# A diagonal LSTM and a small quantum-circuit layer: chunks that come back as one buffer per image, and one store cut into nine

## The chip, the cores and the metric

The kernel runs on one core of one Trainium2 chip. The metric is the device time in microseconds (us) of one execution, the median of three runs. A core has five engines that run their own instruction streams: PE (TensorE, matmuls), DVE (VectorE), ACT (ScalarE), POOL (GpSimd) and SP (SyncE, which here only issues transfers). Transfers between DRAM and the on-chip memory are carried out by 16 DMA engines that serve all issuing queues; here SP's queue (hardware descriptors) and POOL's queue (software descriptors) are used.

## The reference, cut to what matters

The input is x of shape 16 images, 128 channels, 64 by 64, in float32. Layer 0 is a diagonal LSTM over a skewed image, layer 1 a per-pixel map with four angles and a fixed 16-state circuit; both have a group norm ahead of them and a residual around them.

```python
# layer 0: rows are shifted against each other, then scanned column by column
x = x + _L0_conv_ref(_gn(x), w_is, b_is, w_ss, b_ss)
# layer 1, for each pixel of _gn(x):
def _L1_conv_ref(x, pre_w, pre_b, q_weights, post_w, post_b):
    N, C, H, W = x.shape
    xf = x.transpose(0, 2, 3, 1).reshape(-1, C)
    xq = xf @ pre_w.T + pre_b              # 128 channels -> 4 angles
    z = _simulate(xq, q_weights)           # 4 numbers per pixel
    out = z @ post_w.T + post_b            # 4 -> 128 channels
    return out.reshape(N, H, W, -1).transpose(0, 3, 1, 2)
x = x + _L1_conv_ref(_gn(x), pre_w, pre_b, q_weights, post_w, post_b)
```

## The kernel before

**Layout.** The 128 channels lie on the 128 partitions. An image is cut into eight chunks of 512 columns (8 rows of 64, 2 KB per partition, 256 KB per chunk), numbered k = 0 to 7. Layer 0 keeps the state of all 16 images in `ring`, which has room for only 40 of the 64 rows of each image. While the scan runs, the finished rows 0 to 23 of every image (chunks k = 0, 1, 2, "low" chunks) are therefore written to a DRAM buffer `low` and their place in `ring` is filled with later rows of x. Chunks k = 3 to 7 are still in `ring` when layer 1 starts; the 48 low chunks (three for each of 16 images) have to come back.

**Layer 1.** `finish` (L1158) ends every chunk: DVE adds the output of the last matmul, a bias and the chunk itself (L1167, in place), and SP stores the result to `out` (L1173). The main loop goes over images b = 1 to 15 (image 0 is done in halves ahead of it). In an iteration PE makes the outputs of the lower half (k = 0 to 3), DVE finishes them, ACT and DVE turn the angles of image b + 2 into sines (`sines`, L1115 to L1120), PE makes `squares` of image b + 1 and the outputs of the upper half (k = 4 to 7), DVE finishes these, and PE makes the angles of image b + 3 (`angles`, L1099), which read all eight chunks of that image in the order k = 4, 6, 2, 0, 5, 7, 3, 1. So the low chunks of image 15 are needed at the end of iteration 12. PE's outputs go through five PSUM banks.

**Loads.** `places` is a list of free chunk buffers. At first it has eight scratch buffers of the scan (`spare`, the first three of them one tile `trio`) and seven new ones (`low0` to `low6`): 15 chunks, images 0 to 4. Eight of them are loaded by SP in the last scan steps (`low_rows`, L983), seven by POOL. After that every chunk that `finish` is through with gives its buffer to the list, chunks of `ring` too; `load(3)` is called after each half image, takes up to three buffers and issues a load of one chunk each on POOL's queue. With two calls per image, 48 chunks have been asked for by the end of image 5. A load may only start when the store that empties its buffer has landed.

**Stores.** `together` (L1176) says how many chunks go out in one store: low chunks singly, k = 3 singly, and the upper chunks two at a time for images 1 to 3, four at a time (1 MB, 8 KB per partition) after that; image 15 goes out in single chunks. All stores stand in SP's queue in program order. Each also waits for the semaphore of the transfer eight before it, so that at most eight of SP's transfers are under way.

Of the kernel before, what the change touches and what calls it, by code (L numbers as in the profile page):

```python
# [11 lines left out]
F32 = mybir.dt.float32  # L12
# [4 lines left out]
P = 128  # L17
NB = 16
# [6 lines left out]
ROWS = 4  # L25
BLOCK = ROWS * NW
CHUNK = 2 * BLOCK
# [4 lines left out]
FEW = 96  # L32
TWICE = 128
LEAST = 128
AHEAD = RING - SLOTS
BAND = NW + 1
NSTEP = BAND + NW + SLOTS - 1
# [45 lines left out]
def kernel(  # L83
# [16 lines left out]
    nc = tc.nc  # L100
    xv = x.rearrange("b c h w -> b c (h w)")
    ov = out.rearrange("b c h w -> b c (h w)")

    const = ctx.enter_context(tc.tile_pool(name="const", bufs=1))
# [6 lines left out]
    ring = const.tile([P, NB, RING * NW], F32, name="ring")  # L111
    NLOW = NH - RING
    NT = NLOW * NW // CHUNK
    low = dram.tile([NB, P, NLOW * NW], F32, name="low")
# [11 lines left out]


    trio = const.tile([P, 3, CHUNK], F32, name="trio")
    spare = [trio[:, i] for i in range(3)]
    spare += [const.tile([P, CHUNK], F32, name=f"spare{i}") for i in range(3, 8)]  # L130
    w_theta = const.tile([P, 128], F32, name="w_theta")
    w_image = const.tile([P, NB, 48], F32, name="w_image")
    b_image = const.tile([P, NB], F32, name="b_image")
# [5 lines left out]
    def place(r):  # L139

        return (r + AHEAD if r < SLOTS else r - SLOTS) * NW

    def block(r):

        return ring[:, :, place(r) : place(r) + BLOCK]
# [18 lines left out]
    with ExitStack() as scan:  # L164
# [55 lines left out]
        def above(v, a, b):  # L220

            v = v[:, 1, 0:1]
            dims = [list(v.ap[0]), [NB - NC, 2], [1, b - a]]
            return bass.AP(v.tensor, v.offset + a - NB, dims)
# [8 lines left out]
        with ExitStack() as prep:  # L233
# [25 lines left out]
            def rows(b):  # L259
                half = SLOTS // 2  # L260
                first = 0 if b else AHEAD
                early = ((first, half - first), (half, half))
                for r, n in (*(early if b < 3 else ((0, SLOTS),)), (SLOTS, AHEAD)):
                    nc.sync.dma_start(
# [6 lines left out]
            def behind(b):  # L271
# [10 lines left out]
                out=qw, in_=q_weights.rearrange("l w a -> (l w a)").partition_broadcast(P)  # L282
            )
            nc.sync.dma_start(out=ring[:, 0, place(0) : place(AHEAD)], in_=xv[0, :, 0 : AHEAD * NW])
            for i in range(2):
# [146 lines left out]
            def cleared():  # L432
                for v in (*hst, *xns, none, cst[:, :, 0:LEAST]):
                    nc.gpsimd.memset(v, 0.0)
                    yield
                nc.gpsimd.memset(eps, EPS)
                nc.gpsimd.tensor_sub(apart_of, ident, group)
                yield
                nc.gpsimd.memset(w_image, 0.0)
                yield  # L440
# [60 lines left out]
            for g in ORDER:  # L501
                first[g] = ps_gate.tile([P, 2, NC], F32, name=f"ps0_{g}", tag="gate")
                for w, rhs in ((w1T, hst[0][:, :, 0 : LEAST // 2]), (w0T, above(hst[0], 0, LEAST // 2))):
                    nc.tensor.matmul(
                        first[g][:, :, 0 : LEAST // 2],
                        lhsT=w[:, g * 128 : (g + 1) * 128],
# [106 lines left out]
        def reach(t):  # L613

            b = columns(t)[1]
            return b + 4 if b < NC else b

        def plain(t):
            a, b = columns(t)
            return b - a <= FEW  # L620
# [5 lines left out]

        def wide(t, least=LEAST):

            a, b = columns(t)[0], reach(t)
            return max(0, min(a, b - least)), max(b, min(NC, a + least))  # L630

        def diagonal(t, band, q, j0, j1):


            r = 2 * j0 + q + AHEAD * (1 - band)
            at = r * NW + t - BAND * band - 2 * j0 - q
# [15 lines left out]
        def apart(op, *groups):  # L652

            for key in groups:
                tc.declare_no_dep(op.ins, group=key, reason="other rows of the ring")
            return op

        def ahead_of(op, band, j1):

            apart(op, "stores", *(f"reload{g}" for g in reloads if band == 0 or 2 * j1 <= AHEAD + 4 * g))  # L660

# [24 lines left out]
        def gate_ps(t):  # L686

            a, b = wide(t, LEAST // 2)
            ps = {} if t else first
# [172 lines left out]
        def step(t, ps):  # L862

            a, b = columns(t)
            few = plain(t)
            a0, b0 = wide(t, LEAST // 2 if few else LEAST)
            w = reach(t)
# [112 lines left out]
        def low_rows(queue, n, v):  # L980
            b, k = n // NT, n % NT
            of = low[b, :, k * CHUNK : (k + 1) * CHUNK]
            queue.dma_start(out=v, in_=of)  # L983

        waiting = []
        with tc.manual_schedule():
# [26 lines left out]
            v = block(NH - ROWS).rearrange("p i (r w) -> p i r w", w=NW)[:, :, :, NW - STRIP :]  # L1013
# [4 lines left out]
            for i, u in enumerate((d, sq)):  # L1018
                u = u.rearrange("p i r w -> p i (r w)")
# [33 lines left out]
    lowp = ctx.enter_context(tc.tile_pool(name="lowp", bufs=1))  # L1053
# [8 lines left out]

    places = list(spare) + [lowp.tile([P, CHUNK], F32, name=f"low{i}") for i in range(7)]
    lows = []

    def load(n):

        while n and places and len(lows) < NT * NB:  # L1070
            v = places.pop(0)
            lows.append(v)
            if len(lows) > 8:
                low_rows(nc.gpsimd, len(lows) - 1, v)
            n -= 1

    def rows_of(b, k):
        if k < NT:
            return lows[NT * b + k]
        at = place(2 * ROWS * k)  # L1080
        return ring[:, b, at : at + CHUNK]

    def half(v, c):

        if c is None:
            return v
        return v[:, c * BLOCK : (c + 1) * BLOCK]
# [71 lines left out]
    def finish(b, h, po, c=None):  # L1159
        for j in range(4):  # L1160
            k = 4 * h + j
            v = rows_of(b, k)
            x1, y, o = half(v, c), po[j], ov[b, :, k * CHUNK : (k + 1) * CHUNK]
            to = v
            if c is not None:
                o, to = o[:, c * BLOCK : (c + 1) * BLOCK], x1
            nc.vector.scalar_tensor_tensor(to, y, b_out, x1, ALU.add, ALU.add)  # L1167
            n = together(b, k) if c is None else 1
            if (k + 1) % n == 0:
                if n > 1:  # L1170
                    at = place(2 * ROWS * (k + 1 - n))
                    o, to = (u[:, at0 : at0 + n * CHUNK] for u, at0 in ((ov[b], (k + 1 - n) * CHUNK), (ring[:, b], at)))
                nc.sync.dma_start(out=o, in_=to)  # L1173
            if c is None or c == 1 and k < NT:
                places.append(v)

    def together(b, k):

        if k < 4 or b == NB - 1:
            return 1  # L1180
        return 2 if b < 4 else 4

    def idle():
# [4 lines left out]
            nc.tensor.matmul(ps, lhsT=w_out, rhs=v, start=True, stop=True)  # L1188

    with tc.manual_schedule():  # L1190
        load(len(places))

        angles(0, 0)
        angles(0, 1, bank(ps_o, "theta0"))
        first = [sines(0, c) for c in range(2)]
        for later in first:
            next(later)

        th = bank(ps_t, "theta1")
        angles(1, 0, th)  # L1200
        for later in first:
            next(later, None)
        squares(0, 0)
        angles(1, 1, th, (0,))
        po = outputs(0, 0, 0)
        angles(1, 1, th, (1,))
        ths[1, None] = th
        finish(0, 0, po, 0)
        squares(0, 1)
        po = outputs(0, 1, 0)  # L1210
        finish(0, 1, po, 0)
        later = sines(1)
        next(later)
        po = outputs(0, 0, 1, (0, 1))
        th = angles(2, parts=(0,))
        po += outputs(0, 0, 1, (2, 3))
        finish(0, 0, po, 1)
        next(later, None)
        po = outputs(0, 1, 1, (0,))
        angles(2, None, th, (1,))  # L1220
        later = sines(2, by=nc.gpsimd)
        next(later)
        load(3)
        po += outputs(0, 1, 1, (1,))
        squares(1)
        po += outputs(0, 1, 1, (2, 3))
        finish(0, 1, po, 1)
        next(later, None)
        for b in range(1, NB):
            po = outputs(b, 0)  # L1230
            if b == 1:
                angles(3)
            later = sines(b + 2, by=nc.gpsimd if b == 1 else nc.vector) if b + 2 < NB else iter(())
            if b == 1:
                next(later)
            finish(b, 0, po)
            load(3)
            if b == 1:
                po = outputs(b, 1)
                finish(b, 1, po)  # L1240
                load(3)
                squares(2)
                next(later, None)
                angles(4)
                continue
            next(later, None)
            if b + 1 < NB:
                squares(b + 1)
            next(later, None)
            po = outputs(b, 1)  # L1250
            finish(b, 1, po)
            load(3)
            if b + 3 < NB:
                angles(b + 3)
            elif b < NB - 1:
                idle()
# [37 lines left out]
```

## Time and profile before

| | us |
|---|---|
| median of 3 runs (lowest, highest) | 1400.34 (1399.78, 1400.67) |
| the profiled execution, its own time | 1399.66 |
| its span, first to last instruction | 1397.8 |
| layer 1, from the first angles matmul to the end of the span | 1277.0 to 1397.8 |
| images 5 to 14, one iteration | 6.33 |
| last DVE instruction ends | 1386.7 |

Over the span PE is busy for 97%, DVE for 70%, ACT for 56%, POOL for 64%. These are averages over two layers with different limits; the change lies in the last 9% of the span. Times inside the kernel are counted from the start of the span, so the run's own time lies about 1.9 us above them. "DMA share" is the mean busy share of the 16 DMA engines; it can stand a little over 1, since a packet's record overlaps the next one's by a few ns. "To landing" is the time from the start of a transfer's issue to the last of its semaphore writes.

### The profile page before, as it was taken

How to read it: one execution, taken by the hardware profiler on the slowest of the kernel's cores; microseconds unless marked ns; L12 is line 12 of the kernel's file. 1: busy time of each engine (PE TensorE's matmuls, PEld its weight loads, DVE VectorE, ACT ScalarE, POOL GpSimd, SP SyncE). 2: the span in 40 equal slices, each digit the busy share in tenths (PEclk: the TensorE clock that was granted, in tenths of full speed). 3: DMA queues.
4: the chain of work that ended last, by engine and by line, in shares of the span. 5: the costliest groups of instructions: out<-in, count | busy, mean ns of one | idle time of the engine just before them, and what ended most of it. 6: DMA issues, size and time to landing. Idle time of an engine off the chain costs nothing. (4 is left out here: it accounts for less than half of the span.)

```text
span 1397.8 us, 19939 instructions
## 1 busy us (share of the span) xinstructions
PE 1351.0 (97%) x6058; PEld 966.6 (69%) x6058; DVE 973.6 (70%) x2520; ACT 786.3 (56%) x1881; POOL 892.6 (64%) x1584
## 2 busy tenths in 40 slices
PE   7789999999999999999999999999999999989996
PEld 6668887777777777767777767777777778886332
DVE  6973565577767775677777776666665566876996
ACT  6765666555555555555555555555555566644331
POOL 3236777766677777777777766777777667764400
PEclk9999999999999999999999999999999999999998
DMA  9940000000000000133333100000000000014998
GB/s 373 417 199 1 2 1 1 1 1 1 1 1 1 1 1 1 60 121 121 121 121 120 61 1 1 1 1 0 1 1 1 1 0 1 1 31 144 382 415 354
DMA packets 52746, 107.02 MB, mean 77 GB/s; under 512 B 3824, under 2 KB 31504, under 8 KB 49568
## 3 DMA queue, kind: packets, MB, share of 16 engines
q1 hardware_dynamic: 49024, 95.17, 18.3%
q0 software_dynamic: 3472, 10.58, 2.0%
q8 instruction: 48, 0.79, 0.2%
q14 instruction: 58, 0.48, 0.1%
q10 hardware_dynamic: 144, 0.01, 0.0%
HBM read 59.61 MB, written 46.14 MB: 76 GB/s over the span
## 5 line engine op out<-in xcount | busy, mean ns | idle before, releaser
L693 PE MATMUL ps<-spare,wxT 128*128 128x512 f32 (+18 forms) x1280 | 479.6, 518 | 0.6 <-POOL spare L684 0.6
L887 DVE TENSOR_TENSOR ps<-ps,both 128x256 f32<-128x256 f32 (+9 forms) x536 | 219.8, 410 | 295.5 <-PE ps L872 291.1
L891 ACT ACTIVATE ps<-ps,bias 128x512 f32<-128x512 f32 (+23 forms) x480 | 279.2, 583 | 219.5 <-DVE ps L887 183.1
L693 PEld LDWEIGHTS ps<-spare,wxT 128*128 128x128 f32 x1280 | 230.9, 190 | 173.2 <-issue 155.5
L872 PE MATMUL ps<-trio,w1T 128*128 128x256 f32 (+14 forms) x1088 | 306.3, 363 | 0.0
L872 PE MATMUL ps<-trio,w0T 128*128 128x256 f32 (+14 forms) x1088 | 305.5, 362 | 0.0
L922 ACT COPY both<-ps 128x256 f32<-128x256 f32 (+9 forms) x536 | 189.6, 356 | 181.0 <-PE ps L872 161.5
L872 PEld LDWEIGHTS ps<-spare,wsT 128*128 128x128 f32 x1088 | 196.0, 190 | 78.8 <-DVE spare L957 30.4
L872 PE MATMUL ps<-spare,wsT 128*128 128x256 f32 (+14 forms) x1088 | 243.6, 365 | 1.6 <-DVE spare L957 1.3
L730 POOL TENSOR_TENSOR ring<-ring,spare 128x256 f32<-128x256 f32 (+15 forms) x375 | 231.4, 643 | 18.3 <-DVE spare L957 18.0
L872 PEld LDWEIGHTS ps<-trio,w1T 128*128 128x128 f32 x1088 | 201.6, 190 | 22.3
L872 PEld LDWEIGHTS ps<-trio,w0T 128*128 128x128 f32 x1088 | 201.1, 190 | 21.2
L684 POOL TENSOR_TENSOR spare<-spare,rstd 128x512 f32<-128x512 f32 (+10 forms) x160 | 170.9, 1068 | 14.2 <-DVE rstd L528 1.7
L678 POOL TENSOR_TENSOR spare<-ring 128x256 f32<-128x256 f32 (+13 forms) x165 | 139.4, 845 | 0.0
L951 ACT ACTIVATE g<-cst 128x256 f32<-128x256 f32 (+20 forms) x320 | 103.0, 368 | 64.2 <-DVE cst L950 63.6
L957 DVE TENSOR_TENSOR spare<-g,ps 128x256 f32<-128x256 f32 (+17 forms) x319 | 105.3, 367 | 44.3 <-ACT g L951 39.4
L720 POOL TENSOR_TENSOR trio<-spare 128x240 f32<-128x240 f32 (+9 forms) x136 | 102.5, 754 | 36.7 <-DVE spare L957 33.1
L672 POOL TENSOR_TENSOR spare<-ring,mean 128x256 f32<-128x256 f32 (+15 forms) x191 | 122.5, 641 | 2.5 <-DVE mean L517 2.0
L891 ACT ACTIVATE g<-ps,bias 128x512 f32<-128x512 f32 (+20 forms) x160 | 97.3, 608 | 27.6 <-DVE ps L887 21.3
L950 DVE TENSOR_TENSOR cst<-cst,ps 128x256 f32<-128x256 f32 (+20 forms) x320 | 104.5, 368 | 5.5
L947 DVE TENSOR_TENSOR ps<-ps,g 128x512 f32<-128x512 f32 (+20 forms) x160 | 95.1, 594 | 18.7 <-ACT g L891 18.5
L939 DVE TENSOR_TENSOR cst<-cst,ps 128x512 f32<-128x512 f32 (+20 forms) x160 | 92.7, 579 | 16.5 <-POOL spare L231 10.9
(385 smaller groups left out, 1172.3 us busy)
## 6 DMA issues: line engine op xcount, KB each, us to landing
ring<-in_x_dram SPq DMA_DIRECT2D x13, 1024.0 KB, 9.8
low<-ring SPq DMA_DIRECT2D x6, 2048.0 KB, 7.6
ring<-in_x_dram SPq DMA_DIRECT2D x6, 2048.0 KB, 8.2
out_dram<-ring SPq DMA_DIRECT2D x11, 1024.0 KB, 9.1
out_dram<-ring SPq DMA_DIRECT2D x37, 256.0 KB, 7.2
trio<-in_x_dram SPq DMA_DIRECT2D x7, 768.0 KB, 7.6
rest<-in_x_dram SPq DMA_DIRECT2D x7, 768.0 KB, 7.8
ring<-in_x_dram SPq DMA_DIRECT2D x18, 256.0 KB, 9.9
```

Source lines behind the costliest of these rows:

```text
L672: op = nc.gpsimd.tensor_sub(by_pairs(xn, 0, j0, j1), x0, over(mean1, j1 - j0))
L678: op = nc.gpsimd.tensor_sub(by_pairs(xn, 1, j0, j1), lower, of)
L684: nc.gpsimd.tensor_mul(v, v, r)
L693: nc.tensor.matmul(ps[g][:, :, a:b], lhsT=wxT[:, g * 128 : (g + 1) * 128], rhs=xns[t % 2][:, :, a:b], start=t > 0, stop=True, skip_group_c ...
L730: op = engine.tensor_add(x1, x1, by_pairs(new, q, j0, j1))
L872: nc.tensor.matmul(out, lhsT=w[:, g * 128 : (g + 1) * 128], rhs=rhs, start=False, stop=True, skip_group_check=True,)
L887: nc.vector.tensor_add(v, v, both[g][:, a:b])
L891: nc.scalar.activation(to[:, :, a:w], ps[g][:, :, a:w], FUNC[g], bias=bias[:, g : g + 1])
L922: nc.scalar.copy(both[g][:, a:b], ps[g][:, 0, a:b])
L950: nc.vector.tensor_add(c[:, q], c[:, q], ig[:, q])
L951: nc.scalar.activation(th[:, q, a:w], c[:, q], AF.Tanh)
L957: nc.vector.tensor_mul(new[:, q, a:v], th[:, q, a:v], act[GO][:, q, a:v])
```

## The change

The scratch buffers are regrouped: five buffers for three chunks each (`trio`, a second `trio1`, `pair` and `last`, and two new tiles `low0` and `low1`), each holding the low chunks of one image. The place of a buffer is handed on as a whole, image b's to image b + 5, when `finish` is through with k = 2 of image b; `ring` chunks are no longer given away. A load brings three chunks at once (6 KB per partition), or two and one for `pair` and `last`; the calls of `load()` after each half image remain, but find at most one free group per image. Low chunks of images 2 to 14 are stored with their buffer, three at once (or two and one). The upper store of image 11 (`EASED`), 1 MB, isn't issued when its chunks are ready: it is cut into nine accesses, the p-th of partitions p, p + 9, p + 18, ... (two of 15 partitions, seven of 14), and one of them is issued behind each of the next nine stores, those of images 12 to 14.

```diff
+EASED = NB - 5
+APART = 9
-    spare = [trio[:, i] for i in range(3)]
-    spare += [const.tile([P, CHUNK], F32, name=f"spare{i}") for i in range(3, 8)]
+    trio1 = const.tile([P, 3, CHUNK], F32, name="trio1")
+    pair = const.tile([P, 2, CHUNK], F32, name="pair")
+    spare = [v[:, i] for v, n in ((trio, 3), (trio1, 3), (pair, 2)) for i in range(n)]
...
-    places = list(spare) + [lowp.tile([P, CHUNK], F32, name=f"low{i}") for i in range(7)]
-    lows = []
-    def load(n):
-        while n and places and len(lows) < NT * NB:
-            v = places.pop(0)
-            lows.append(v)
-            if len(lows) > 8:
-                low_rows(nc.gpsimd, len(lows) - 1, v)
-            n -= 1
+    later = [lowp.tile([P, NT, CHUNK], F32, name=f"low{i}") for i in range(2)]
+    last = lowp.tile([P, CHUNK], F32, name="last")
+    first_lows = spare + [last] + [v[:, i] for v in later for i in range(NT)]
+    groups = {i: [(v, NT)] for i, v in ((0, trio), (1, trio1), (3, later[0]), (4, later[1]))}
+    groups[2] = [(pair, 2), (last.unsqueeze(1), 1)]
+    freed, loaded, parted = [], [len(groups)], []
+    def load():
+        while freed and loaded[0] < NB:
+            b = loaded[0]
+            groups[b] = freed.pop(0)
+            k = 0
+            for v, n in groups[b]:
+                of = low[b, :, k * CHUNK : (k + n) * CHUNK]
+                nc.gpsimd.dma_start(out=v, in_=of.rearrange("p (k n) -> p k n", n=CHUNK))
+                k += n
+            loaded[0] += 1
+    def low_group(b, k):
+        for v, n in groups[b]:
+            if k < n:
+                return v, n, k
+            k -= n
...
             n = together(b, k) if c is None else 1
-            if (k + 1) % n == 0:
+            if (k + 1) % n == 0 if k >= NT else n == 1 or n == low_group(b, k)[2] + 1:
                 if n > 1:
-                    at = place(2 * ROWS * (k + 1 - n))
-                    o, to = (u[:, at0 : at0 + n * CHUNK] for u, at0 in ((ov[b], (k + 1 - n) * CHUNK), (ring[:, b], at)))
-                nc.sync.dma_start(out=o, in_=to)
-            if c is None or c == 1 and k < NT:
-                places.append(v)
+                    o = ov[b, :, (k + 1 - n) * CHUNK : (k + 1) * CHUNK]
+                    if k < NT:
+                        o, to = o.rearrange("p (k n) -> p k n", n=CHUNK), low_group(b, k)[0]
+                    else:
+                        at = place(2 * ROWS * (k + 1 - n))
+                        to = ring[:, b, at : at + n * CHUNK]
+                if n > 1 and k >= NT and b == EASED:
+                    pieces = [(o[p::APART], to[p::APART]) for p in range(APART)]
+                    parted.extend(pieces)
+                else:
+                    nc.sync.dma_start(out=o, in_=to)
+                    if parted:
+                        o, to = parted.pop(0)
+                        nc.sync.dma_start(out=o, in_=to)
+            if k == NT - 1 and (c is None or c == 1):
+                freed.append(groups[b])
     def together(b, k):
-        if k < 4 or b == NB - 1:
+        if b == NB - 1 or k == NT:
             return 1
+        if k < NT:
+            return low_group(b, k)[1] if b > 1 else 1
         return 2 if b < 4 else 4
...
-        load(len(places))
+        for n in range(len(spare), len(first_lows)):
+            low_rows(nc.gpsimd, n, first_lows[n])
...
-            load(3)
+            load()
```

In the built programs the instruction streams of PE, DVE and ACT hold the same work in the same order, and the scan's waits are the same. SP's transfers in layer 1 go from 97 stores to 82 (nine of them the pieces), POOL's loads from 40 to 20.

More of the change, by code (lines that the diff above doesn't have):

```diff
@@ L1061 @@
     ths, turns, sqs = {}, {}, {}
-    places = list(spare) + [lowp.tile([P, CHUNK], F32, name=f"low{i}") for i in range(7)]
-    lows = []
-    def load(n):
-        while n and places and len(lows) < NT * NB:
-            v = places.pop(0)
-            lows.append(v)
-            if len(lows) > 8:
-                low_rows(nc.gpsimd, len(lows) - 1, v)
-            n -= 1
+    later = [lowp.tile([P, NT, CHUNK], F32, name=f"low{i}") for i in range(2)]
[19 more added lines that the diff above has]
+            k -= n
     def rows_of(b, k):
         if k < NT:
-            return lows[NT * b + k]
+            v, _, i = low_group(b, k)
+            return v[:, i]
         at = place(2 * ROWS * k)
@@ L1236 @@
             finish(b, 0, po)
-            load(3)
+            load()
             if b == 1:
@@ L1240 @@
                 finish(b, 1, po)
-                load(3)
+                load()
                 squares(2)
@@ L1251 @@
             finish(b, 1, po)
-            load(3)
+            load()
             if b + 3 < NB:
```

## The prediction

> **What bounds the kernel now.** I read first the page's slices, which show where the transfers are heavy.
>
> ```profile
> span 1397.8 us, 19939 instructions
> DVE  6973565577767775677777776666665566876996
> DMA  9940000000000000133333100000000000014998
> GB/s 373 417 199 1 2 1 1 1 1 1 1 1 1 1 1 1 60 121 121 121 121 120 61 1 1 1 1 0 1 1 1 1 0 1 1 31 144 382 415 354
> ```
>
> Only the last three slices (35 us each) bear on this change: there DVE and the DMA engines are full together. Next, windows of layer 1's end (PE, PEld, DVE, ACT, POOL busy, PE clock, DMA share, GB/s).
>
> ```profile
> 1344.00:1386.00 42.00, 40.59 (x201) 13.50 (x200) 41.04 (x66) 12.41 (x21) 0.00 (x0) 0.99 1.03 413
> ...
> 1392.00:1393.00 1.00, 0.00 (x0) 0.00 (x0) 0.00 (x0) 0.00 (x0) 0.00 (x0) 0.50 0.91 344
> 1393.00:1394.00 1.00, 0.00 (x0) 0.00 (x0) 0.00 (x0) 0.00 (x0) 0.00 (x0) 0.50 0.26 98
> 1394.00:1395.00 1.00, 0.00 (x0) 0.00 (x0) 0.00 (x0) 0.00 (x0) 0.00 (x0) 0.50 0.07 27
> 1395.00:1396.00 1.00, 0.00 (x0) 0.00 (x0) 0.00 (x0) 0.00 (x0) 0.00 (x0) 0.50 0.06 25
> ```
>
> DVE works 98% of 1344 to 1386 and ends at 1386.7; the stores run on to 1396.1. A share of 0.06 is one DMA engine of 16: twelve engines end by 1393.2, three by 1394.2, and one alone writes two more us. Its last semaphore write is at 1396.5. So two limits lie one behind the other: the compute chain, 6.33 us an image, and behind it 9.8 us in which the late engine drains. Then the chain's last row and SP's last wait:
>
> ```profile
> 1385.39 1.32 DVE ring L1167 x2
> ```
> ```profile
> SPq L1290 <- DMA out_dram<-ring: 4.6, 1, 4.6
> ```
>
> Last, the transfers by window, 1300 to 1345 and then 1345 to 1398 (KB each, us to landing):
>
> ```profile
> low<-low POOLq DMA_DIRECT2D x7, 256.0 KB, 7.8
> out_dram<-low SPq DMA_DIRECT2D x7, 256.0 KB, 12.2
> out_dram<-trio SPq DMA_DIRECT2D x3, 256.0 KB, 15.4
> ```
> ```profile
> out_dram<-ring SPq DMA_DIRECT2D x28, 256.0 KB, 7.2
> out_dram<-low SPq DMA_DIRECT2D x7, 256.0 KB, 7.9
> ```
>
> While loads run beside them, stores land 12 to 15 us after issue, later 7 to 8. The last load of before is issued early:
>
> ```profile
> 1336.53 1.06 POOL L983 DMA_DIRECT2D ring<-low  x2 [3.02 <-DMA out_dram<-ring]
> ```
> ```profile
> 1365.61 1.92 PE L1099 MATMUL theta_None<-ring,w_image 128*32 128x512 f32 x16
> 1367.47 1.91 PE L1149 MATMUL po_None<-sq,w_out 32*128 32x512 f32 x8
> ```
>
> It lands at 1344.8, and image 15's angles read it at 1365.6: today no load is ever waited for.
>
> **The change, part by part.** *Fewer, longer packets.* In the trace's packet records a 2 KB row takes 84 ns, 4 KB 159, 8 KB 309, so 6 KB is an estimate of 234, on the line between. Three 2 KB rows cost 252. Each engine carries 8 of 128 rows: ten triple stores save 10 x 8 x 18 ns = 1.44 us on every engine, three pairs (168 to 159) 3 x 8 x 9 = 0.22. POOL's packets already hold two rows in 159 ns, so a triple load saves 4 ns a row, 9 x 8 x 4 = 0.29. Each transfer also writes a 4-byte packet of 9 ns per engine: 15 SP and 20 POOL transfers fewer, 0.3. Sum 2.25 us on each engine. Bounds: 1.1 if only half a packet's 9 ns fixed part is real time (records overlap), 2.25 if all is. It counts on the path while the engines are never idle, as from 1300 on. If compute sets the end, it is worth nothing.
>
> *The nine accesses.* A normal 1 MB store puts 8 packets of 309 ns on each engine, 2.47 us. Accesses of 15 and 14 rows can't reach all 16 engines. For the one late engine the price lies between -2.47 us (left out of all nine) and +0.31 (a row of each, nine for eight). No row shows which engine is late. [...] Nine more issues on SP at 0.33 us each lie between stores that come 0.66 us apart or more; SP's window of eight transfers then holds only four stores or so for images 12 to 14, which is enough where landing takes 7 us and three stores leave per 6.33 us.
>
> [...]
>
> *Loads later.* This is what the change adds to the path. Before, six chunks were asked for per image and all were back by 1344.8. Now one image is asked for per image, and image 15's load waits for image 10's low store. In before's times that chain is: image 10's k = 2 ends on DVE at 1351.9 (five periods of 6.33 back from image 15's); its store lands after 7.9 us (window without loads) to 12.2 (with); the load lands after about 7 (6.5 to 7.8 in the rows of `low` loads over layer 1; the triple's further 0.5 MB is three chunks on one semaphore, as deep as the queue of single chunks it replaces). Needed: the first low chunk is the third of eight in `angles`, so 0.46 us after 1365.6, and PE has 0.85 us in hand (its next outputs are done near 1367.9, DVE takes them at 1368.8), so 1366.9. Low end: 1351.9 + 7.9 + 6.5 = 1366.3, not late. High end: 1351.9 + 12.2 + 7.8 = 1371.9, 5 us late. I take 3, nearer the row with loads, because loads now run until then. Behind the waiting matmuls stand the outputs of image 13, and DVE waits for those; DVE has 2% of slack and doesn't catch up. So DVE ends at 1386.7 + 3.0 = 1389.7. POOL's queue holds nothing else, so its own waits hurt nobody.
>
> *Sum.* Compute: 1389.7 + 3.5 = 1393.2 for the last semaphore write. The 3.5 lies between 2.0 (a 256 KB store on idle engines: issued 1292.5, first landing 1294.6) and 9.8 (now), near the low end as the backlog shrinks: image 13 to 15 make 2 MB each 6.33 us, which is 5.0 us of transfer at 413 GB/s. Transfers alone: 1396.5 - 2.25 - 2.47 = 1391.8, the three middling engines 1394.4 - 2.25 + 0.31 = 1392.4. The later counts: 1393.2, that is 3.3 us sooner. 1399.66 becomes 1396.4 for an execution like the profiled one; the median stands 0.7 above that one, so 1397.0.
>
> **The rivals.** *A: as above*, 1397.0, own range 1394.0 to 1397.6. The low end is no late load and compute alone as the limit: 1386.7 + 3.5 = 1390.2, 6.3 sooner than now.
>
> *B: the gain is eaten, no change that can be told.* Either the late engine isn't one that is left out: 1396.5 - 2.25 + 0.31 = 1394.6, which gives 1398.4. Or loads are 5 us late: 1391.7 + 3.5 = 1395.2, 1399.0. I price B at 1398.7. For it: one engine of 16, and stores that take 12.2 us beside loads. Against it: 1.03 DMA share without a gap, on which every saved packet counts.
>
> *C: slower, the ring of five groups starves.* A load can't start before the store in its own buffer has landed, and this store stands in SP's queue behind upper stores of 1 MB. With the 15.4 us of the `trio` row, and three chunks that share the engines with stores (7.8 for the first, 1.3 for each further one at half of 413 GB/s), image 15's load lands at 1351.9 + 15.4 + 10.4 = 1377.7, 10.8 us late; 1386.7 + 10.8 + 3.5 = 1401.0, 4.5 later than now: 1404.8. It decides from 9.1 us of lateness on (1396.5 + 2.8 - 3.5 - 1386.7). Against it: a waiting PE makes no stores, so the queue ahead of the load drains meanwhile.
>
> **How the numbers follow.** A 0.50, B 0.33, C 0.17. About 0.2%, 2.8 us, is what a measurement of this kernel can tell from no change: faster is below 1397.5, slower above 1403.1. A lies mostly below, B between, C above, so the chances are A's, B's and C's. The forecast is A's 1397.0. The range runs from 1394.0 (no late load) to 1403.5: B whole and the near side of C, whose far part and a small part below A are left out.
>
> **What would show it.** Right, if packets of 6 KB take about 234 ns; if the DMA share falls from 1.0 to 0 within about a us at the end, with no engine alone for 2 us; if the angles of images 12 to 15 wait for a load on POOL's queue, some 3 us in all, and DVE ends near 1389.7, the last landing some 3.5 us later. Wrong, if DVE still ends at 1386.7 (loads in time, then faster than 1396), if one engine still ends 2 us alone (B), or if PE's wait grows from image to image past 9 us (C). The scan up to 1277 should be unchanged; a difference there would be none of these steps.

## The result, and the profile after

The changed kernel takes 1403.11 us (median of 13 runs, 1402.35 to 1410.34) against 1399.91 us before (13 runs), a ratio of 1.003 with a 95% interval of 1.0023 to 1.0037. It is 3.2 us slower, where 2.9 us faster than 1399.91 was forecast. The range held the time, the sign was wrong.

The profiled execution took 1402.46 us. First the page's slices, 40 of 35 us each: DMA is the busy share of the 16 engines in tenths.

```profile
span 1400.7 us, 19848 instructions
DMA  9940000000000000133333100000000000004998
GB/s 369 417 201 1 2 1 1 1 1 1 1 1 1 1 1 1 60 121 120 120 121 120 61 1 1 1 1 1 1 1 1 1 0 1 9 24 154 388 413 337
```

Up to the end of the scan the slices are as before, within a few GB/s. The last one moves 337 GB/s where before it moved 354, over a span that is 2.9 us longer. The windows of layer 1's end tell where (busy time of PE, PEld, DVE, ACT, POOL, then clock, DMA share, GB/s), before and after:

```profile
1368.00:1374.00 6.00, 6.00 (x27) 2.01 (x23) 5.97 (x11) 2.03 (x4) 0.00 (x0) 1.00 1.03 413
1374.00:1380.00 6.00, 6.00 (x24) 2.09 (x24) 5.97 (x10) 1.09 (x2) 0.00 (x0) 1.00 1.03 410
1380.00:1386.00 6.00, 4.59 (x17) 1.56 (x16) 5.24 (x9) 0.00 (x0) 0.00 (x0) 0.92 1.02 409
```
```profile
1368.00:1374.00 6.00, 6.00 (x33) 2.02 (x33) 5.63 (x10) 2.40 (x4) 0.00 (x0) 1.00 0.93 349
1374.00:1380.00 6.00, 6.00 (x33) 2.01 (x26) 5.39 (x9) 1.77 (x3) 0.00 (x0) 1.00 0.83 319
1380.00:1386.00 6.00, 6.00 (x24) 1.95 (x23) 5.97 (x10) 1.71 (x3) 0.00 (x0) 1.00 0.87 351
1386.00:1392.00 6.00, 6.00 (x21) 2.24 (x20) 5.24 (x9) 0.00 (x0) 0.00 (x0) 1.00 0.97 362
...
1397.00:1398.00 1.00, 0.00 (x0) 0.00 (x0) 0.00 (x0) 0.00 (x0) 0.00 (x0) 0.50 1.00 385
1398.00:1399.00 1.00, 0.00 (x0) 0.00 (x0) 0.00 (x0) 0.00 (x0) 0.00 (x0) 0.50 0.42 160
```

Two things changed. The DMA engines, full before, now have gaps from 1368 to 1386. And DVE, which ended at 1386.7, works on to 1394.5. No engine drains alone any more: the share falls from 1.00 to 0 within 1.1 us. DVE is late because PE waits for loads, which it never did before (the waits: engine, tile, line, what was waited for, us in total, times, longest):

```profile
PEld theta_None L1117 <- DMA low<-low: 3.8, 4, 1.5
PEld theta_None L1117 <- DMA trio<-low: 2.5, 4, 0.9
```

The chain in order of time (start, duration, what) shows one such wait, image 13's load; the timeline of POOL's queue shows image 15's, the last:

```profile
1351.43 0.33 issue
1351.75 7.99 DMA low<-low
1359.74 0.04 issue
1359.78 1.91 PE theta_None L1117 x12
```
```profile
1366.22 0.53 POOL L1083 DMA_DIRECT2D trio<-low  x1 [7.89 <-DVE near_None L1135]
```

A load goes out and PE takes up the angles 8 us later, the moment it has landed. Image 15's load leaves at 1366.2, when by the prediction it had to be back at 1366.9.

One correction before runs are compared. The start differs from execution to execution: from 100 us of the span on, everything comes 0.1 to 1.6 us later in the twelve other profiles than in that of before (the new kernel: 0.6). The shift arises ahead of the scan and stays the same through it. The kernel before with only its store of image 11 changed has it too (1.4 in e2), so it is not put down to the change; what it comes from is open. In what follows, DVE's lateness and the table have this shift taken off, so that times count as in the profile of before; profile lines stand as they are.

DVE's lateness by image, first instruction of the image's lower half against before: images 1 to 3 none, 4 and 5 0.5 us, 6 2.0, 7 2.4, 8 3.2, 9 3.6, 10 4.6, 11 6.0, 12 6.5, 13 7.1, 14 and 15 7.2. It grows image by image.

### The profile page after: what moved, and what is told of

It reads as the page before. It is cut to its first block, busy times and chain, and to the rows that moved or that the text cites. A ratio compares the mean times of both kernels' runs of the same rounds, so it can differ in the third digit from the quotient of the medians.

```text
span 1400.7 us, 19848 instructions
## 1 busy us (share of the span) xinstructions
PE 1357.1 (97%) x6058; PEld 967.5 (69%) x6058; DVE 975.1 (70%) x2520; ACT 786.6 (56%) x1881; POOL 883.2 (63%) x1564
## 5 line engine op out<-in xcount | busy, mean ns | idle before, releaser
L696 PE MATMUL ps<-trio,wxT 128*128 128x512 f32 (+18 forms) x1280 | 479.6, 517 | 0.6 <-POOL trio L687 0.6
L696 PEld LDWEIGHTS ps<-trio,wxT 128*128 128x128 f32 x1280 | 230.9, 190 | 173.2 <-issue 155.5
L875 PEld LDWEIGHTS ps<-pair,wsT 128*128 128x128 f32 x1088 | 196.0, 190 | 78.8 <-DVE pair L960 30.4
L875 PE MATMUL ps<-pair,wsT 128*128 128x256 f32 (+14 forms) x1088 | 243.5, 365 | 1.6 <-DVE pair L960 1.3
L733 POOL TENSOR_TENSOR ring<-ring,pair 128x256 f32<-128x256 f32 (+15 forms) x375 | 231.8, 645 | 18.2 <-DVE pair L960 18.1
L687 POOL TENSOR_TENSOR trio<-trio,rstd 128x512 f32<-128x512 f32 (+10 forms) x160 | 171.1, 1069 | 14.2 <-DVE rstd L531 1.7
L681 POOL TENSOR_TENSOR trio<-ring 128x256 f32<-128x256 f32 (+13 forms) x165 | 139.9, 848 | 0.0
L960 DVE TENSOR_TENSOR pair<-g,ps 128x256 f32<-128x256 f32 (+17 forms) x319 | 105.5, 368 | 44.1 <-ACT g L954 39.2
L723 POOL TENSOR_TENSOR trio<-pair 128x240 f32<-128x240 f32 (+9 forms) x136 | 102.8, 756 | 36.6 <-DVE pair L960 33.0
L675 POOL TENSOR_TENSOR trio<-ring,mean 128x256 f32<-128x256 f32 (+15 forms) x191 | 122.9, 643 | 2.8 <-DVE mean L520 2.2
L953 DVE TENSOR_TENSOR cst<-cst,ps 128x256 f32<-128x256 f32 (+20 forms) x320 | 104.6, 368 | 5.5
```

What stands on the lines that cost most here:

```text
L675: op = nc.gpsimd.tensor_sub(by_pairs(xn, 0, j0, j1), x0, over(mean1, j1 - j0))
L681: op = nc.gpsimd.tensor_sub(by_pairs(xn, 1, j0, j1), lower, of)
L687: nc.gpsimd.tensor_mul(v, v, r)
L696: nc.tensor.matmul(ps[g][:, :, a:b], lhsT=wxT[:, g * 128 : (g + 1) * 128], rhs=xns[t % 2][:, :, a:b], start=t > 0, stop=True, skip_group_c ...
L733: op = engine.tensor_add(x1, x1, by_pairs(new, q, j0, j1))
L875: nc.tensor.matmul(out, lhsT=w[:, g * 128 : (g + 1) * 128], rhs=rhs, start=False, stop=True, skip_group_check=True,)
```

## The experiments

The middle columns come from one profile each: DVE's end, the last store packet, the time that the engines were busy on the mean from 1283 to that packet, and idle in two stretches (sums over the packet records, divided by 16, with overlaps of records taken off; good to some 0.3 us). The last column is the median less that of the kernel before in the same comparison. The ratios in the text are not made from these medians and can differ from them by 0.0004.

| | DVE ends | last packet | busy | idle 1368 to 1386 | idle after 1386 | median, us against before |
|---|---|---|---|---|---|---|
| before | 1386.7 | 1396.1 | 104.6 | 0.2 | 2.9 | 0 |
| changed | 1393.9 | 1398.5 | 105.8 | 2.6 | 1.1 | +3.2 |
| e1, no accesses | 1393.5 | 1396.4 | 105.0 | 1.5 | 0.7 | +1.6 |
| e2, before + nine accesses | 1386.7 | 1396.6 | 104.8 | 1.9 | 0.7 | +1.9 |
| e3, seven groups, accesses | 1386.7 | 1395.5 | 104.3 | 1.5 | 1.2 | +0.5 |
| e4, seven groups, no accesses | 1386.7 | 1394.8 | 103.4 | 0.1 | 2.9 | -1.4 |
| e5, before + eight of 16 rows | 1386.7 | 1396.0 | 105.7 | 1.1 | 0.7 | +1.0 |
| e6, before + two of 64 rows | 1386.8 | 1396.2 | 104.5 | 0.7 | 2.5 | +0.3 |
| e7, six groups, no accesses | 1390.2 | 1395.0 | 104.0 | 0.1 | 1.7 | -0.5 |
| e8, eight groups, no accesses | 1386.7 | 1393.6 | 103.6 | 0.1 | 1.6 | -1.4 |
| e9, before + nine by POOL | 1386.7 | 1395.7 | 105.3 | 0.8 | 1.0 | +0.3 |
| e10, before, 15 places | 1393.1 | 1395.9 | 105.0 | 1.3 | 0.5 | +1.1 |
| e11, e8 again | 1386.7 | 1394.0 | 103.1 | 0.0 | 2.4 | -1.8 |

**e1 to e4: each part alone, and more room.** e1 is the changed kernel with image 11's upper store whole:

```diff
-EASED = NB - 5
+EASED = NB
```

> The changed kernel, but image 11's upper store goes out whole as it did before. Theory (five groups handed on five images ahead make the loads late, and DVE ends about 7 us later for it): PE still waits for the loads of images 10 to 15, DVE ends between 1393 and 1396, and the time is within 2.5 us of the changed kernel's 1403.1. Rival (the nine accesses, with their issues between the stores, cost the time): DVE ends near 1387 to 1390 and the time falls below 1400.

e2 is the kernel before with nothing but the nine accesses:

```diff
+                if n > 1 and k >= NT and b == EASED:
+                    parted.extend((o[p::APART], to[p::APART]) for p in range(APART))
+                else:
+                    nc.sync.dma_start(out=o, in_=to)
+                    if parted:
+                        o, to = parted.pop(0)
+                        nc.sync.dma_start(out=o, in_=to)
```

> The kernel before with nothing but the nine accesses for image 11's upper store. If the one engine that ends last is among those that an access of 14 or 15 rows leaves out, its end moves from 2 us after the others to about level with them: 1.5 to 2.5 us less than before. If it is not left out, nothing to 0.4 us more. DVE's end stays at 1386.7 either way. If the accesses hold up SP: more than 0.5 us slower.

e3 keeps the accesses and gives the loads two groups more, `ring` chunks 4 to 6 of images 0 and 1, so that image 15 takes over image 8's buffer and not image 10's; e4 is e3 with the whole store.

```diff
+            if k == 6 and b in (0, 1) and (c is None or c == 1):
+                freed.append([(ring[:, b, 0 : NT * CHUNK].rearrange("p (k n) -> p k n", n=CHUNK), NT)])
```

> The changed kernel with two more groups: chunks 4 to 6 of images 0 and 1 in the ring are handed on too, so a group goes to the image seven on, not five. Theory (depth of the hand-on is what is late): PE waits for no load, DVE's end comes back to 1387 to 1388 (0.6 us of that is the scan's, if it repeats), the last landing near 1392, the time 1396 to 1398, faster than both. Rival (the three-chunk transfers are late by themselves): the loads are still waited for and the time stays above 1401.

> Seven groups and image 11's upper store whole. Theory: DVE ends as with seven groups and the nine accesses, 1387 to 1388; the end differs by the late engine alone: about 1394.3 (1396.5 less the 2.2 us of packets), so 1 to 2.5 us more than with the accesses. If the accesses do not relieve the late engine: the same as with them or less.

Measured: e1 1401.02, ratio 1.0013 [1.0003, 1.0022]; e2 1401.32, 1.0015 [1.0005, 1.0024]; e3 1399.97, 1.0002 [0.9992, 1.0011]; e4 1398.03, 0.9991 [0.9982, 1.0]. The accesses cost 1.9 us on the kernel before (e2), 1.9 with seven groups (e3 less e4) and 1.6 with five (changed less e1). They relieve nothing. Room is worth 3.0 us (e1 less e4): with seven groups no load is waited for and DVE ends where it did. The windows of e1 and of e4 show the room at work without the accesses:

```profile
1374.00:1380.00 6.00, 6.00 (x37) 2.01 (x29) 5.97 (x11) 2.40 (x4) 0.00 (x0) 1.00 0.99 401
1380.00:1386.00 6.00, 6.00 (x25) 2.17 (x24) 5.97 (x10) 1.72 (x3) 0.00 (x0) 1.00 0.81 328
```
```profile
1374.00:1380.00 6.00, 6.00 (x25) 2.14 (x24) 5.97 (x10) 1.31 (x3) 0.00 (x0) 1.00 1.01 417
1380.00:1386.00 6.00, 5.60 (x19) 1.75 (x18) 5.24 (x9) 0.00 (x0) 0.00 (x0) 1.00 1.03 429
```

In e1 DVE comes 7 us late, so the backlog of stores that had kept the engines full runs out: the share is 0.81 in 1380 to 1386. In e4 it is 1.03 there, and the bytes flow at 417 and 429 GB/s in these two windows against 410 and 409 before. That is what the longer packets give where the engines are never idle.

**e5 and e6: why do nine accesses cost 1.9 us?** The kernel before with the same edit as e2, and `APART = 8`, then `APART = 2`.

> The kernel before with image 11's upper store cut into eight accesses of 16 rows (every eighth partition) instead of nine of 15 and 14. [...] Theory S (slots: SP keeps at most eight transfers under way, and a piece of a ninth of a MB takes a slot as a whole MB does, so the queue behind runs dry and engines stand idle): about 1.7 us over before, nearly what nine accesses cost (1.9), and gaps in the DMA share between 1374 and 1386. Rival U (uneven engines: 14 of 16 carry nine packets where a whole store gives them eight, and the late one is among these): no cost, within 0.4 us of before, and no gaps.

> The kernel before with image 11's upper store cut into two accesses of 64 rows (every second partition), each issued behind one of the next two stores. Theory S (slots): two slots for 1 MB in place of one, so the cost falls to about a seventh of that of eight pieces, 0.2 us or so, within 0.5 us of before. Rival U (uneven engines): no cost either. Rival M (that the store is moved behind others is what costs): the same cost as with eight pieces, since the first piece leaves as late.

Measured: e5 1400.15, ratio 1.0011 [1.0002, 1.002]; e6 1399.5, 1.0002 [0.9993, 1.0011]. Eight pieces of 16 rows cost 1.0, neither theory's figure; two cost nothing that can be told, so moving the store behind two others costs little by itself. If 16 rows reach all 16 engines, which no record shows since none names an engine, the unevenness of nine explains at most half of their 1.9. SP's timeline of e2 showed something else (start, duration of the issue; L1181 issues the accesses, L1178 the other stores), and e5's below it:

```profile
1372.13 0.49 SPq L1178 DMA_DIRECT2D out_dram<-ring  x1
1372.68 0.81 SPq L1181 DMA_DIRECT2D out_dram<-ring  x1
1373.59 0.48 SPq L1178 DMA_DIRECT2D out_dram<-ring  x1
1374.13 0.82 SPq L1181 DMA_DIRECT2D out_dram<-ring  x1
1375.05 0.48 SPq L1178 DMA_DIRECT2D out_dram<-ring  x1
1375.58 0.82 SPq L1181 DMA_DIRECT2D out_dram<-ring  x1
```
```profile
1374.02 0.50 SPq L1181 DMA_DIRECT2D out_dram<-ring  x1
1374.73 0.42 SPq L1178 DMA_DIRECT2D out_dram<-ring  x1
1375.20 0.50 SPq L1181 DMA_DIRECT2D out_dram<-ring  x1
```

Issuing one access of 14 rows takes SP 0.82 us, one of 16 rows 0.50, a whole store 0.33 at the least (before). In e2 SP does nothing but issue from 1372 to 1384: a store and an access, 0.37 MB, every 1.45 us, 260 GB/s, where the engines had been taking 410. They run dry: their share is 0.93 and 0.86 in the windows from 1374 and 1380, where it was 1.03 and 1.02 before.

```profile
1374.00:1380.00 6.00, 6.00 (x24) 2.07 (x24) 5.97 (x10) 1.66 (x3) 0.00 (x0) 1.00 0.93 358
1380.00:1386.00 6.00, 5.94 (x20) 1.94 (x18) 5.24 (x8) 0.00 (x0) 0.00 (x0) 1.00 0.86 319
```

Theory S, the window of eight transfers, is not what holds e2: after 1372 none of SP's waits there is for a landing. In e5 it has a part. SP's own waits from 1371.5 to 1384 in e5 hold these lines:

```profile
SPq L1181 <- DMA out_dram<-ring: 1.1, 2, 0.9
SPq L1181 <- DMA out_dram<-low: 0.2, 1, 0.2
SPq L1178 <- DMA out_dram<-low: 0.2, 1, 0.2
```

So in e5 SP stood for 1.5 us until an earlier transfer had landed, as S said, besides the dearer issues. How its 1.0 us divides between the two is not shown.

The rows show in the records too: e2 has 112 more 4-byte packets than before, which is 2 x 15 + 7 x 14 less the 16 of the whole store; the changed kernel's SP queue has 1296 from 1277 us on, 16 for each of its 73 whole stores and 128 for the pieces. Why an issue of 14 rows takes 0.82 us and one of 16 rows 0.50 no run here shows.

**e9: the accesses off SP.** As e2, with the nine issued by POOL's queue.

```diff
-                        nc.sync.dma_start(out=o, in_=to)
+                        nc.gpsimd.dma_start(out=o, in_=to)
```

> The kernel before with the same nine accesses of 15 and 14 rows, issued at the same places by POOL's queue instead of SP's (POOL has no other work there). Theory I (issue: in the run with nine accesses SP took 0.82 us to issue each, back to back with the stores between, 1.45 us for a pair of 0.37 MB, which is 260 GB/s against the 410 the engines had been doing, so the engines stood idle for 1.9 us between 1368 and 1386): with SP free of them the share stays near 1.0 there and the cost of 1.9 us falls to 0.5 or less; about 1399.5. Rival U (uneven engines: some carry nine packets, some none): the cost stays, 1.5 to 2 us over before.

Measured: 1399.7, ratio 1.0001 [0.9993, 1.001], as the theory of the issue had it. The shares are 0.98 and 0.97 in place of e2's 0.93 and 0.86:

```profile
1374.00:1380.00 6.00, 6.00 (x25) 2.09 (x24) 5.97 (x10) 1.45 (x3) 0.00 (x0) 1.00 0.98 381
1380.00:1386.00 6.00, 5.74 (x20) 1.90 (x18) 5.24 (x9) 0.00 (x0) 0.00 (x0) 1.00 0.97 381
```

More than one thing changed with the queue, though. POOL stands behind none of SP's stores and had eight accesses out by 1368.3, and the pieces take none of SP's eight places:

```profile
1363.97 4.30 POOL L1181 DMA_DIRECT2D out_dram<-ring  x8 [25.50 <-DVE ring L1169]
```

So e9 shows that the cost goes when SP doesn't issue the pieces, and not how much of it each of these is worth. That SP's issue time is the cause in e2 rests on both: on e9, and on e2's rows, in which SP issues without a pause while the engines run dry.

**e7, e8 and e11: how much room?** e4's edit for image 1 alone (six groups), and for images 0, 1 and 2 (eight).

> The changed kernel without the nine accesses and with one group more (the ring chunks 4 to 6 of image 1 are handed on to image 7), so that image b's low place goes to image b + 6 in the end. Theory L (loop: store landing and load need about 34 us, five images give 31.65, six 38.0): no late load, DVE ends as with seven groups, 1398.0 us, 3 us under the five groups. Rival D (every group less costs alike, 1.5 us each): half-way between five and seven groups, 1399.5 us.

> The changed kernel without the nine accesses and with three groups more (ring chunks 4 to 6 of images 0, 1 and 2). Theory L: nothing left to gain from depth, as seven groups, 1398.0 us within 0.5. Rival D: 1396.5 us. A third way: the loads come earlier and stand closer together among the first stores, which then land later, while SP's end stays: again 1398.0.

> The eight groups once more, with whole upper stores, to learn whether they beat the kernel before. If the gain of the longer packets is real (work of the engines 1.8 us less, no load late): 1.4 us under before, ratio 0.9990. If the first result was chance: ratio 1.0.

Measured: six groups 1398.71, ratio 1.0001 [0.9992, 1.0011]; eight 1397.76, 0.9992 [0.9983, 1.0001], and again 1397.58, 0.9987 [0.9978, 0.9996]. In DVE's end theory L fell: six groups are 3.4 us late, half of five's 7, as D had it. But the time went 2 us down from five groups to six, less than 1 to seven, and nothing clear further: lateness was paid only where it let the engines run dry, and with six groups they don't (idle 0.1), as e7's row shows beside e1's 0.81 above:

```profile
1380.00:1386.00 6.00, 6.00 (x26) 2.04 (x24) 5.21 (x8) 1.08 (x2) 0.00 (x0) 1.00 1.01 413
```

L's fixed loop of 34 us was wrong as well. With more room DVE is further ahead of the transfers, and a load waits longer for the store in its buffer: from DVE's last instruction on image b's third chunk to the issue of the load 7 to 9 us with five groups, 10 to 12 with six, 11 to 15 with seven and eight.

**e10: the room of five groups without the groups.** The kernel before hands on only its 15 low buffers.

```diff
-            if c is None or c == 1 and k < NT:
+            if k < NT and (c is None or c == 1):
```

> The kernel before, but only the 15 low chunks' buffers are handed on, as in the changed kernel with its five groups, and not the ring's; loads and stores stay single chunks. Theory B (buffers: with five images of room the loads come 7 us late by the end, and the stores behind them dry up; grouping has no part in it): DVE ends 5 to 8 us later than in before, and the run is 2 to 3 us over before, 1401.5 to 1402.5. Rival T (the triple is late because three chunks hang on one store and one semaphore): loads in time or nearly, DVE's end within 2 us of before's, and the run within 0.5 us of before.

Measured: 1400.47, ratio 1.0006 [0.9997, 1.0015]. Single chunks wait as triples do:

```profile
PEld theta_None L1099 <- DMA low<-low: 6.3, 5, 2.4
PE theta_None L1099 <- DMA low<-low: 2.1, 3, 1.5
```

DVE ends 6.3 us late against 6.8 in e1. So what makes loads late is that `ring` chunks no longer go back to the list, and grouping adds about half a us. The theory of the triple fell by the lateness; the theory of buffers put 2 to 3 us on the time, and it was 1.1, with no change still inside the interval.

## Why the prediction was wrong

**The step that failed: "Loads later ... I take 3".** The prediction priced the last link alone, image 10's buffer to image 15, and started it with image 10 on time ("image 10's k = 2 ends on DVE at 1351.9"). The price of the link was not the error: from that instruction to the landing it took 18.0 us (1366.9 + 3 - 1351.9), and the run shows 16.5, 9.2 to the load's issue at 1366.2 and 7.3 to its landing. But image 10's store left here:

```profile
1357.07 0.33 SPq L1199 DMA_DIRECT2D out_dram<-trio  x1
```

That is 5.2 us after the forecast's 1351.9, 0.6 of it the later start of the execution. The rest is that every load from image 6's on, all but image 7's, had been waited for, 0.3 to 1.5 us each. By the list of lateness above, in which image j's load shows at image j - 2, the loads of images 5 to 9 cost 2.4 us, those of 10 to 14 another 4.1, and image 15's, the only one that was priced, 0.7. A wait isn't made up later, as the prediction itself said, so it had to be added over all the loads.

**The second: "The nine accesses", at -2.47 us.** Three pairs of runs give +1.6 to +1.9 (the changed kernel and e1 by medians of different comparisons), outside both bounds. These weighed what an engine carries. No run shows the -2.47: no record names the engine of a packet, and that the late one is left out of all nine was the author's assumption. What the runs show in its place is a cost that goes when SP doesn't issue the pieces (e9, +0.3), and there "Nine more issues on SP at 0.33 us each" took 0.82 us for 14 rows, beside stores that had to come as fast as the engines drain. The forecast that no engine ends alone came true, but it doesn't speak for an engine left out: e5, which has no piece of 14 or 15 rows, ends so too (share 0.96, 0.11 and 0.00 in the us from 1396, 1397 and 1398). Where engines had run dry none ended alone (e1, e2, e5, e10: idle 0.5 to 0.7 us after 1386, against 2.9 before). Which engine it is, and so whether nine accesses leave it out, stays open.

**The packets.** The size was right, 234 ns by the median of 6 KB packets. Of the 2.25 us, e4, e8 and e11 show 1.0 to 1.5 us of busy time, nearer the bound of 1.1. How much of a packet's 9 ns fixed part is real time no run tests by itself. In the changed kernel nothing is left of it. Its engines were busy 1.2 us longer than before: 8 KB packets from 1368 to 1390 took 340 ns on the mean, 313 before, and POOL's packets took 1.7 us per engine more with five groups than with seven (28.7% of 1300 to 1345 and 14.9% of 1345 to 1400 in e1, 30.9% and 9.9% in e4).

**The tail.** 3.5 us after DVE's end was forecast to the last semaphore write. To the last packet it was 2.8 to 2.9 where DVE is late and the accesses are absent (e1, e10), and 4.6 with them, 4.9 to the last semaphore write. So DVE's 1386.7 + 7.2, the 0.6 of the execution's start and 4.9 from there make 1399.4 for the last semaphore write, against the forecast's 1393.2: 4.2 us by the loads, 1.4 by the tail, 0.6 by the start.

**The rivals.** C had the sign, and of the mechanism the store that a load waits for and PE's wait that grows from image to image. But it too priced the last link alone: 25.8 us from 1351.9 to 1377.7, where the link took 16.5, and the lateness of 10.8 us that it made of this was 7.2, added up over the loads of eleven images. Its point of decision, 9.1 us, came too late, since it kept the tail of 3.5 us and took the accesses for free. B's two conditions, an engine that ends alone and loads only 5 us late, did not come.

**What the change could have been.** With eight groups and whole stores the regrouping gains: 0.9987 [0.9978, 0.9996], 1.8 us under before, and some 5 us under the changed kernel by medians of different comparisons. It beats both.

## What to carry to other kernels

Where buffers go round, price the whole chain of hand-ons from the first one, not the last link: each load that comes late delays the store that the next one waits for, and what set it here was how many buffers circulate (single chunks in five images of room came 6.3 us late, e10), far more than whether they go singly or by threes (6.8, e1). Here a wait cost only where it let the saturated resource run dry (e1, share 0.81, against e7, 1.01), so read the transfer share after the wait, not the wait alone. And count the issuing queue as a resource of its own: here a piece of 14 rows took 0.82 us to issue and a whole store 0.33 at the least, and in e2 SP issued 260 GB/s where the engines had been moving 410.

## What was not expected of the hardware

An issue on SP took 0.33 us at the least for 128 partitions, 0.50 for 16 and 0.82 for 14; most of the whole stores between the pieces took 0.34 to 0.55, some up to 1.6. Four of the last five stores of before, after DVE's end, took 0.6 to 1.1 us to issue with six or seven transfers under way, and others 0.33 with seven under way; what makes the difference no run shows. So one long issue doesn't by itself show a dear transfer; 0.82 again and again, with DMA engines idle (shares of 0.93 and 0.86 in e2), does. And one DMA engine, 2 to 3 us behind the rest at the end of before (e4 and e6 show it too), was no loss while others had gaps: in e2 the gaps grew by 1.7 us between 1368 and 1386 and the idle time at the end shrank by 2.2.
